# A conv-attention and mixture-of-experts network on one core: the order of the last norm, of the late expert blocks, of the last additions and of the first matmuls

## The chip, the cores and the metric

The kernel runs on one core of a Trainium2 chip. The metric is the device time of one execution in microseconds (us). A core has a matmul engine (TensorE, PE in the profile; its weight loads are PEld), three engines for elementwise work (VectorE is DVE, ScalarE is ACT, GpSimd is POOL) and SyncE (SP), which only issues DMA transfers here. Each engine works through its own queue in order, and waits on semaphores for the others.

## The reference

The input `x` is 8 images of 256 channels and 32 x 32 = 1024 positions (tokens). All is float32.

```python
# layer 0, for each image, 8 heads of 64
qkv = xt @ w_qkv + b_qkv
attn = softmax(q @ k^T * 64**-0.5, axis=query)
t = (attn @ v) @ w_out + b_out + xt
# layer 1
n = layernorm(t)                       # over the 256 channels
t = t + softmax((n @ W^T) @ n^T) @ n   # 1024 x 1024 scores
n = layernorm(t)
gates = top 2 of softmax(n @ router_w^T), normed to sum 1
y = n + sum over 8 experts of gate_e * (gelu(n @ w1[e] + b1[e]) @ w2[e] + b2[e])
out = t + y                            # turned back to channels
```

## The kernel before

The images go one after the other. `layer0` computes the first layer of an image in 32 steps, each of one pair of heads and one block of 128 keys: scores into PSUM (`psc`), two maxima on DVE (`first_max`, `second_max`), the exponential on ACT (`soften`), the values divided by the sums on DVE (`divide`, which writes `vs`), and the product with the values into `po` (`gather_values`). Between PE's parts of a product stand empty instructions on another queue (`relay`): on POOL's for image 0, on SP's for the others. Then `pr` multiplies by `w_out` and adds to the residual `t1`, which `residual` has made of the input (turned on DVE) and the bias (added on POOL).

`attend` is the second attention. It norms `t1` into `n1` (class `Norm`: statistics block by block, square root on ACT, reciprocal, writes), turns `n1` to channels (`to_channels`: PE transposes and two DVE copies), and mixes eight blocks of queries; at named places it calls `fill`, where other work is put in. `normed` does the second norm and its turn.

The experts are handled in two ways. For images 0 to 6 each token's normed row is scattered to its two experts' lists in DRAM (`dispatch`, one scatter in a step of the next image's layer 0). After layer 0 of image 7, `experts` runs 63 blocks of 256 rows: `fetch` loads a block (SP), `stage` copies its weights (ACT), `turned` transposes it (`xb`, DVE), `hidden` multiplies by `w1` (`ph`) and applies gelu, `collect` multiplies by `w2` (`pe`), adds the bias, scales by the gate and scatters the rows to `y` (POOL). Two buffers hold `xb`, four hold weights. The last four blocks are handed to `fill` and finished within image 7's attention. Image 7's own experts are computed in `dense`: for each of 8 experts and 2 halves of the tokens, `pdh`, gelu, `pdy`, and four gated adds to `t2` on DVE.

Beside `dense`, `Results` ends the other seven images: 14 halves, for each of which a sum and two results are loaded (512 KB each), added on DVE (`add`), transposed on DVE into one of two buffers `oT` and stored (`store`). `tick`, called after each dense step, stores the half added before and adds the next:

```python
def tick(self, k, behind):
    if self.stored < self.added:
        self.store()
    if self.added < len(self.todo):
        self.add(behind)
```

The order on each engine is set by a scheduler with a cost model of its own; `tc.issue_after(x)` places what is issued within it behind the instruction `x` in the order, and `add_manual_dep` makes it wait.

At the start the first input halves and weights are loaded, three idle matmuls run, and `Begin.all` computes the values of six token blocks (`pv`, two contraction halves `cc` each), with small PE transposes of biases and routers (`ps_bqk`, `ps_W`, `ps_r`, `ps_rs`, `ps_b1`) between.

## Time and profile before

| | us |
|---|---|
| median of 3 runs | 2308.49 (2308.31 to 2310.03) |
| the profiled execution's own time | 2309.37 |
| its span in the profile | 2307.6 |
| PE busy | 2248.4 |
| DVE busy | 1567.6 |
| ACT busy | 1238.8 |
| POOL busy | 313.6 |

The span is that of the instructions; the execution's own time takes in what lies around it. In lines of the timeline the columns are start, duration, engine, line, operation, out<-in, count, and in brackets the idle time before it with what ended it. In lines of waits they are the waiting engine and line, what it waited for, total us, times, longest. Counts of matmuls are of records: a float32 matmul leaves two.

### The profile page before, as it was taken

What the parts mean: (1) busy time and instruction counts of PE and PEld (TensorE: products, weight loads), DVE (VectorE), ACT (ScalarE), POOL (GpSimd) and SP (SyncE); (2) the same over time, 40 slices, a digit from 0 to 9 for tenths busy, and PEclk for the clock granted to TensorE, in tenths of its full rate; (3) what the DMA queues carried; (4) which work ended last, traced back from release to release, by engine and by line L of the source; (5) the groups of instructions that cost most, each with busy time, mean ns of one, the idle gap of its engine ahead of it and who ended that gap; (6) DMA issues with size and microseconds to landing.
All of it is one profiled execution on the core that took longest, in us unless ns stands there. A gap on an engine that the chain in (4) does not pass through costs nothing.

```text
span 2307.6 us, 38039 instructions
## 1 busy us (share of the span) xinstructions
PE 2248.4 (97%) x13061; PEld 1213.5 (53%) x13061; DVE 1567.6 (68%) x3922; ACT 1238.8 (54%) x2221; POOL 313.6 (14%) x313
## 2 busy tenths in 40 slices
PE   9999999999999999999999999999999989999996
PEld 3345633563456335643554355534553468885664
DVE  4776688557865786578757775677668955556575
ACT  3664566356635663656474656466446645556311
POOL 1000012000200030003000200021001225551100
PEclk9999999999999999999999999999999999999998
DMA  8996201020103010201021101100050146651475
GB/s 277 356 348 189 50 17 40 7 57 11 47 1 63 6 52 1 45 19 52 6 37 27 45 13 21 43 20 20 14 123 17 40 86 147 147 143 42 167 216 156
DMA packets 277177, 182.82 MB, mean 79 GB/s; under 512 B 194564, under 2 KB 232247, under 8 KB 275960
## 3 DMA queue, kind: packets, MB, share of 16 engines
q1 hardware_dynamic: 264264, 150.08, 24.3%
q0 software_dynamic: 11632, 29.78, 3.6%
q8 instruction: 104, 1.70, 0.3%
q14 instruction: 89, 0.73, 0.1%
q10 hardware_dynamic: 1088, 0.52, 0.1%
HBM read 63.47 MB, written 106.61 MB: 74 GB/s over the span
## 4 chain that ended last, share of the span: by engine, by line
PE 83%; DVE 5%; ACT 5%; SPq 4%; issue 2%; DMA 1%; POOL 0%; DVEq 0%; ACTq 0%; POOLq 0%
PE po L587 19%; PE psc L510 19%; PE pqk L380 7%; PE py L897 7%; PE pr L689 5%; PE pv L417 4%; PE ph L1332 3%; PE ps L791 3%; PE pe L1359 3%; PE pdy L1547 2%; PE px L728 2%; PE pdh L1524 2%; SPq L880 2%; PE pqk L358 2%; PE ps1z L791 2%
## 5 line engine op out<-in xcount | busy, mean ns | idle before, releaser
L551 ACT ACTIVATE ex<-psc,nmax 128x1024 f32<-128x1024 f32 x512 | 570.0, 1114 | 301.4 <-DVE scrap L534 218.5
L510 PE MATMUL psc<-qk,qk 64*64 64x512 f32 x4096 | 576.0, 592 | 4.3 <-ACT ex L551 4.1
L587 PE MATMUL po<-ex,vs 64*64 64x512 f32 x4096 | 570.6, 591 | 3.5 <-DVE vs L567 2.4
L534 DVE TENSOR_SCALAR_CACHE_REDUCE scrap<-psc,nmax 128x512 f32<-128x512 f32 x512 | 384.4, 751 | 158.7 <-PE psc L510 130.5
L525 DVE TENSOR_REDUCE nmax<-psc 128x1 f32<-128x512 f32 x512 | 350.6, 685 | 9.3 <-PE psc L510 9.3
L510 PEld LDWEIGHTS psc<-qk,qk 64*64 64x64 f32 x4096 | 179.7, 132 | 281.8 <-ACT ex L551 133.1
L587 PEld LDWEIGHTS po<-ex,vs 64*64 64x64 f32 x4096 | 175.0, 132 | 277.5 <-DVE vs L567 82.9
L1149 POOL DMA_INDIRECT rows<-n,d_at x112 | 109.1, 974 | 515.8 <-DVE nmax L525 479.8
L380 PE MATMUL pqk<-xT,wqkv 128*128 128x512 f32 x384 | 171.2, 599 | 0.0
L1380 POOL DMA_INDIRECT y<-yb,to x126 | 123.6, 981 | 191.7 <-DVE yb L1374 165.4
L345 ACT ACTIVATE qk<-pqk,b_qks 128x512 f32<-128x512 f32 x124 | 85.5, 690 | 88.9 <-PE pqk L380 79.8
L417 PE MATMUL pv<-wqkv,xT 128*128 128x512 f32 x256 | 121.7, 600 | 2.2 <-ACT wqkv L121 1.3
L380 PEld LDWEIGHTS pqk<-xT,wqkv 128*128 128x128 f32 x384 | 71.0, 190 | 99.9 <-issue 77.3
L1332 PE MATMUL ph<-xb,w_ring 128*128 128x256 f32 x488 | 117.2, 384 | 4.5 <-DVE xb L1321 4.5
L880 ACT COPY spare<-home 32x256 f32<-32x256 f32 x272 | 109.4, 402 | 17.4 <-DVE home L868 11.9
L689 PE MATMUL pr<-wo,res 128*128 128x256 f32 x512 | 113.6, 383 | 2.0 <-ACT res L606 2.0
L897 PE MATMUL py<-n,spare 128*128 128x256 f32 x512 | 114.9, 379 | 0.0
L1141 POOL IOTA n<- 128x8 f32 x14 | 2.0, 142 | 829.6 <-PE py L897 829.6
L1359 PE MATMUL pe<-w_ring,hb 128*128 128x256 f32 x472 | 111.6, 379 | 0.0
L689 PEld LDWEIGHTS pr<-wo,res 128*128 128x128 f32 x512 | 98.4, 192 | 19.6 <-ACT res L606 6.0
L897 PEld LDWEIGHTS py<-n,spare 128*128 128x128 f32 x512 | 96.5, 190 | 20.1 <-issue 4.3
L1332 PEld LDWEIGHTS ph<-xb,w_ring 128*128 128x128 f32 x488 | 93.6, 192 | 18.5 <-DVE xb L1321 5.7
(262 smaller groups left out, 2795.2 us busy)
## 6 DMA issues: line engine op xcount, KB each, us to landing
rows<-zero SPq DMA_DIRECT2D x7, 8256.0 KB
xr<-rows SPq DMA_DIRECT2D x252, 64.0 KB
xs<-in_x_dram SPq DMA_DIRECT2D x64, 128.0 KB
ys<-y SPq DMA_DIRECT2D x16, 512.0 KB
spare<-home SPq DMA_DIRECT2D x240, 32.0 KB
out_dram<-oT SPq DMA_DIRECT2D x60, 128.0 KB
xT<-in_x_dram SPq DMA_DIRECT2D x7, 1024.0 KB
sums<-t SPq DMA_DIRECT2D x7, 1024.0 KB
```

Source lines behind the costliest of these rows:

```text
L380: mm = nc.tensor.matmul(pq[:, ts(n, 512)], wqkv[:, cc, t, ts(g, P)], xT[:, cc, ts(n, 512)], start=(cc == 0), stop=(cc == NCC - 1),)
L417: nc.tensor.matmul(pv, self.xT[:, cc, ts(i, P)], wqkv[:, cc, 2, :], start=(cc == 0), stop=(cc == NCC - 1),)
L510: mm = nc.tensor.matmul(pss[at, h][ts(c, DK), ts(n, 512)], k[r, j * P + c * DK : j * P + (c + 1) * DK], q[r, ts(n, 512)], start=True, stop ...
L525: firsts[at, h] = nc.vector.tensor_reduce(nmax, pss[at, h][:, ts(0, 512)], AX.X, ALU.max, negate=True)
L534: seconds[h] = nc.vector.tensor_scalar(scrap, pss[at, h][:, ts(1, 512)], -1.0, nmaxes[at, h], ALU.mult, ALU.min, accum_out=nmax,)
L551: nc.scalar.activation(ex, pss.pop((at, h)), AF.Exp, bias=nmaxes.pop((at, h)), scale=1.0, accum_out=sums[at][:, h : h + 1],)
L587: mm = nc.tensor.matmul(po[n][ts(h, DK), :], vss[at][keys, h, :], exps[at, h][keys, ts(n, 512)], start=(j == 0 and turn == 0), stop=(j == ...
L689: nc.tensor.matmul(pr[:, :C], res[g][:, ts(i, P)], wo[:, g, :], start=(g == 0), stop=(g == NPAIR - 1))
L880: move(to[ts(k, SQ), a], since[ts(a, SQ), k])
L897: evicted["mixed"] = nc.tensor.matmul(py[:, :D], aT[m], n1[:, m, :], start=(m == 0), stop=(m == NT - 1))
L1332: last = nc.tensor.matmul(ph[:, ts(fc, BR)], wb[:, dc * FF + fc * P : dc * FF + (fc + 1) * P], xb[:, dc, :], start=(dc == 0), stop=(dc == ...
L1359: mm = nc.tensor.matmul(py[:, ts(r, D)], hT[:, fc, ts(r, P)], wb[:, ts(fc, D)], start=(fc == 0), stop=(fc == NFC - 1),)
```

## The change

1. Start: the `cc = 0` matmuls of all six `pv` blocks are issued first, and the transposes of `b_rows` and `W_rows` are placed behind them.
2. `residual`: POOL's bias add is cut into two halves, each behind the `divide` of one of the two following steps, for every image.
3. Last attention: its norm is no longer done before `attend` but in 23 steps, one behind each of the first expert blocks (four empty, eight of statistics, square root, one empty, reciprocal, eight writes). Weight copies are placed behind the last gelu, and before there is one, behind the last copy of `res`.
4. Late blocks: block `end - 2` is finished before the last turn of the attention instead of at the second norm. Of block `end - 1` the bias add stays there, and the scaling and scatters come behind the norm's two copies to channels; POOL's adds of the normed tokens come behind the scaling.
5. Dense stage: a tick adds a half and transposes and stores it at once, behind the step's gated adds, and the next step's gated adds are placed behind that transpose. The last half of image 7 is transposed and stored in two parts.

```diff
+    bigs = [big(f"pv_0_{i}") for i in range(0, 6, 2)]
+    first_pvs = [bigs[i // 2][:, ts(i % 2, 512)] for i in range(6)]
+    for i, pv in enumerate(first_pvs):
+        opened = nc.tensor.matmul(
+            pv, next_x[:, 0, ts(i, P)], wqkv[:, 0, 2, :], start=True, stop=False
+        )
...
-        nc.tensor.transpose(ps[:, ts(t, NPAIR)], b_rows[:, t, :], ident[:NPAIR, :NPAIR])
+        with tc.issue_after(opened.ins):
+            nc.tensor.transpose(ps[:, ts(t, NPAIR)], b_rows[:, t, :], ident[:NPAIR, :NPAIR])
...
-        nc.gpsimd.tensor_add(t1, t1, b_o.unsqueeze(1).to_broadcast([P, NT, C]))
-        return t1
+        def bias(n, behind):
+            some = t1[:, ts(n, NB), :]
+            added = nc.gpsimd.tensor_add(some, some, b_o.unsqueeze(1).to_broadcast([P, NB, C]))
+            tc.add_manual_dep(added.ins, behind.ins.name, BEHIND)
+
+        return t1, [lambda behind, n=n: bias(n, behind) for n in range(NH2)]
...
                 with tc.issue_after(seconds[0].ins):
                     ahead = divide(at - 1) if at > 0 else seconds[0]
+                    if parts and at > 0:
+                        parts.pop(0)(ahead)
...
-        tick("turned", to_channels(tokens, nT, f"n2_{b}"))
+        copied = to_channels(tokens, nT, f"n2_{b}")
+        tick("turned", copied)
...
+            with tc.issue_after(copied.ins):
+                fill("turned")
...
-                    tc.add_manual_dep(added.ins, written.ins.name, BEHIND)
+                    tc.add_manual_dep(added.ins, evicted["scaled"].ins.name, BEHIND)
...
         def stage(b):
+            with tc.issue_after((gelus[-1] if gelus else evicted["copied"]).ins):
+                copy_weights(b)
...
                 collect(b - 4, hiddens.pop(b - 4), last, squares)
+                if steps:
+                    with tc.issue_after(evicted["scaled"].ins), tc.issue_after(gelus[-1].ins):
+                        steps.pop(0)()
...
-        def tick(self, k, behind):
-            if self.stored < self.added:
-                self.store()
+        def tick(self, behind):
             if self.added < len(self.todo):
-                self.add(behind)
+                self.store(self.add(behind))
...
+        def part(at):
+            turned = nc.vector.transpose(
+                oT[:, :, ts(at, P // parts)].rearrange("p g (i t) -> p i g t", i=some),
+                total[:, ts(at, some), :].rearrange("p i (g c) -> p i g c", c=SQ),
+            )
+            for a in range(NQ):
+                queue = nc.scalar if b == B - 1 and a % 2 else nc.sync
+                queue.dma_start(
+                    dst[n, a][:, :, ts(at, P // parts)], oT[ts(a, SQ), :, ts(at, P // parts)]
+                )
+            return turned
...
+                with tc.issue_after(others.last.ins) if others.last else nullcontext():
+                    for j in range(2):
...
+                if (e, n) == (E - 1, NH2 - 1):
+                    if i == 0:
+                        ending = store(b, t2[:, ts(n, NB), :], n, 2)
+                    with tc.issue_after(added.ins):
+                        others.last = ending(i // 2)
+            others.tick(added)
+            if (e, n) == (E - 1, 0):
+                with tc.issue_after(added.ins):
+                    others.last = store(b, t2[:, ts(n, NB), :], n)
...
+        n1 = one.tile([P, NT, D], F32, tag="n", name=f"n1_{b}")
+        n1_norm = Norm(t1, n1, 1e-5, f"a{b}")
+        steps = [lambda: None for _ in range(4)]
+        steps += [lambda i=i: n1_norm.stats(i, i + 1) for i in range(NT)]
+        steps.append(lambda: n1_norm.root(0, NT))
+        steps.append(lambda: None)
+        steps.append(lambda: n1_norm.invert(0, NT))
+        steps += [lambda i=i: n1_norm.write(i, i + 1) for i in range(NT)]
+        product, result = experts(groups[0], evicted["divided"], table, steps)
...
+            elif place == "last weights 2":
+                result(end - 2)
             elif place == "norm 2":
                 with tc.issue_after(evicted["mixed"].ins):
-                    result(end - 2)
-                    result(end - 1)
+                    sends = result(end - 1, False)
+            elif place == "turned":
+                for send in sends:
+                    evicted["sent"] = send()
```

More of the change, by code (lines that the diff above doesn't have):

```diff
@@ L220 @@
         for dc in range(NCC):
-            nc.tensor.transpose(
-                ps[:, dc * D + ec * P : dc * D + (ec + 1) * P], W_rows[:, ec, ts(dc, P)], ident
-            )
+            with tc.issue_after(opened.ins):
+                nc.tensor.transpose(
+                    ps[:, dc * D + ec * P : dc * D + (ec + 1) * P], W_rows[:, ec, ts(dc, P)], ident
+                )
     WT = const.tile([P, NCC, D], F32, name="WT")
@@ L268, in __init__, with stats @@
             self.rstd = small.tile([P, NT], F32, tag="rstd", name=f"rstd_{name}")
-        def blocks(self, first, end):
-            t, mv, rstd = self.t, self.mv, self.rstd
+        def stats(self, first, end):
+            t, mv = self.t, self.mv
             for i in range(first, end):
@@ L277, in blocks, with root, write @@
                 nc.vector.bn_aggr(mv[:, i, :], st)
-            some = rstd[:, first:end]
+        def root(self, first, end):
+            mv, some = self.mv, self.rstd[:, first:end]
             nc.vector.tensor_scalar_add(some, mv[:, first:end, 1], self.eps)
             nc.scalar.activation(some, some, AF.Sqrt)
-            nc.vector.reciprocal(some, some)
+        def write(self, first, end):
+            t, mv, rstd = self.t, self.mv, self.rstd
             for i in range(first, end):
@@ L295, in blocks, with invert @@
             return written
+        def invert(self, first, end):
+            some = self.rstd[:, first:end]
+            nc.vector.reciprocal(some, some)
+        def blocks(self, first, end):
+            self.stats(first, end)
+            self.root(first, end)
+            self.invert(first, end)
+            return self.write(first, end)
     def layer_norm(t, dst, eps, name):
@@ L402, in __init__, with open, product @@
             self.todo = list(range(NT))
+        def open(self):
+            if self.v is None:
+                self.v = one.tile([P, NT, INNER], F32, tag="v", name=f"v_{self.b}")
+        def product(self, pv, i, cc):
+            return nc.tensor.matmul(
+                pv,
+                self.xT[:, cc, ts(i, P)],
+                wqkv[:, cc, 2, :],
+                start=(cc == 0),
+                stop=(cc == NCC - 1),
+            )
         def values(self, n, single=False):
             b = self.b
-            if self.v is None:
-                self.v = one.tile([P, NT, INNER], F32, tag="v", name=f"v_{b}")
+            self.open()
             now, self.todo = self.todo[:n], self.todo[n:]
@@ L416, in values @@
                 for cc in range(NCC):
-                    nc.tensor.matmul(
-                        pv,
-                        self.xT[:, cc, ts(i, P)],
-                        wqkv[:, cc, 2, :],
-                        start=(cc == 0),
-                        stop=(cc == NCC - 1),
-                    )
+                    self.product(pv, i, cc)
             for i, pv in zip(now, pvs):
@@ L437, in at, with all @@
                     self.project(True)
-            if place not in ("between 2", "last products"):
+            if place not in ("between 2", "last weights 2", "last products", "turned"):
                 self.values(1)
-        def all(self):
-            for _ in range(3):
-                self.values(2)
+        def all(self, pvs):
+            self.open()
+            now, self.todo = self.todo[: len(pvs)], self.todo[len(pvs) :]
+            for i in now:
+                self.product(pvs[i], i, 1)
+            for i in now:
+                nc.vector.tensor_add(self.v[:, i, :], pvs[i], b_v)
             for _ in range(2):
@@ L501, in layer0 @@
         po, copied, counted = None, None, None
+        parts = []
         def score(at, h, n):
@@ L611, in gather_values @@
                 ]
+                evicted["copied"] = copied[-1]
             return mm
@@ L671, in layer0 @@
                     with tc.issue_after(ahead.ins):
-                        t1 = residual(b, xs)
+                        t1, parts = residual(b, xs)
                 if g == 0:
@@ L693, in layer0, with attend @@
         return t1
-    def attend(b, t1, fill, tick=nothing):
+    def attend(b, t1, fill, tick=nothing, n1=None):
         spare = [
@@ L703, in attend @@
         SQ_AT = {1: (3, None), 2: (0, 7), 3: (1, 6), 4: (0, 1), 5: (4, 7), 6: (5, 6)}
-        n1 = one.tile([P, NT, D], F32, tag="n", name=f"n1_{b}")
-        layer_norm(t1, n1, 1e-5, f"a{b}")
+        if n1 is None:
+            n1 = one.tile([P, NT, D], F32, tag="n", name=f"n1_{b}")
+            layer_norm(t1, n1, 1e-5, f"a{b}")
         fill("norm 1")
@@ L951, in attend @@
         mix(*sixth)
+        fill("last weights 2")
         now = turn_now(7, eighth[1])
@@ L1248, in plan, with experts @@
         yield placed
-    def experts(group, behind, table):
+    def experts(group, behind, table, steps):
         n = group.n
@@ L1285, in experts, with copy_weights @@
         spare = two.tile([P, LATE // 2, WE], F32, tag="xT", name="w_late")
-        firsts, seconds = {}, {}
+        firsts, seconds, gelus = {}, {}, []
         W1 = NCC * FF
         def stage(b):
+            with tc.issue_after((gelus[-1] if gelus else evicted["copied"]).ins):
+                copy_weights(b)
+        def copy_weights(b):
             late = b - (group.nb - LATE // 2)
@@ L1342, in hidden @@
             for fc in range(NFC):
-                nc.scalar.activation(
-                    hT[:, fc, :],
-                    ph[:, ts(fc, BR)],
-                    AF.Gelu,
-                    bias=b1T[:, bass.ds(at + fc, 1)],
-                    scale=1.0,
+                gelus.append(
+                    nc.scalar.activation(
+                        hT[:, fc, :],
+                        ph[:, ts(fc, BR)],
+                        AF.Gelu,
+                        bias=b1T[:, bass.ds(at + fc, 1)],
+                        scale=1.0,
+                    )
                 )
@@ L1366, in collect, with add @@
             yb = two.tile([P, R, D], F32, tag="yb", name=f"yb_{n}_{b}")
-            with tc.issue_after(squares.ins) if squares else nullcontext():
-                nc.vector.tensor_add(
+            def add():
+                return nc.vector.tensor_add(
                     yb,
@@ L1372, in collect, with send @@
                 )
+            if squares is not None:
+                with tc.issue_after(squares.ins):
+                    add()
+                    send(b, yb)
+            return mm, add, yb
+        def send(b, yb):
+            if True:
                 where = wheres.pop(b)
-                nc.vector.tensor_mul(yb, yb, where[:, :, 0:1].to_broadcast([P, R, D]))
+                scaled = nc.vector.tensor_mul(yb, yb, where[:, :, 0:1].to_broadcast([P, R, D]))
+                evicted["scaled"] = scaled
                 to = small.tile([P, R], I32, tag="to", name=f"to_{n}_{b}", bufs=4)
@@ L1379, in collect @@
             for r in range(R):
-                nc.gpsimd.indirect_dma_start(
+                sent = nc.gpsimd.indirect_dma_start(
                     out=group.ways[R * b + r][:, :],
@@ L1387, in collect @@
                 )
-            return mm
+            return sent
         rows, hiddens, wheres = {}, {}, {}
@@ L1403, in experts @@
                 collect(b - 4, hiddens.pop(b - 4), last, squares)
+                if steps:
+                    with tc.issue_after(evicted["scaled"].ins), tc.issue_after(gelus[-1].ins):
+                        steps.pop(0)()
+        assert not steps
         for b in range(group.nb - LATE, group.nb - LATE // 2):
@@ L1409, in product, with result @@
             return mm
-        def result(b):
-            return collect(b, hiddens.pop(b), None, None)
+        def result(b, whole=True):
+            mm, add, yb = collect(b, hiddens.pop(b), None, None)
+            if whole:
+                add()
+                return send(b, yb)
+            return add, lambda: send(b, yb)
         return product, result
@@ L1434, in __init__ @@
             self.sent, self.added, self.stored = 0, 0, 0
+            self.last = None
             for _ in self.slots:
@@ L1455, in add, with store @@
                 for k in range(2):
-                    nc.vector.tensor_add(total, total, self.slots[at][:, k])
-        def store(self):
+                    added = nc.vector.tensor_add(total, total, self.slots[at][:, k])
+            return added
+        def store(self, behind):
             at = self.stored % len(self.slots)
@@ L1461, in store @@
             self.stored += 1
-            store(self.group.items[n], self.totals[at], h)
+            with tc.issue_after(behind.ins):
+                self.last = store(self.group.items[n], self.totals[at], h)
             self.load()
-        def tick(self, k, behind):
-            if self.stored < self.added:
-                self.store()
+        def tick(self, behind):
             if self.added < len(self.todo):
-                self.add(behind)
-    def store(b, total, n):
+                self.store(self.add(behind))
+    def store(b, total, n, parts=1):
         oT = two.tile([P, D // SQ, P], F32, tag="qk1", name=f"oT_{b}_{n}")
-        nc.vector.transpose(
-            oT.rearrange("p g (i t) -> p i g t", i=NB),
-            total.rearrange("p i (g c) -> p i g c", c=SQ),
-        )
         dst = out[b].rearrange("(g c) (n a k) -> n a c g k", c=SQ, n=NH2, a=NQ)
-        for a in range(NQ):
-            queue = nc.scalar if b == B - 1 and a % 2 else nc.sync
-            queue.dma_start(dst[n, a], oT[ts(a, SQ)])
+        some = NB // parts
+        def part(at):
+            turned = nc.vector.transpose(
+                oT[:, :, ts(at, P // parts)].rearrange("p g (i t) -> p i g t", i=some),
+                total[:, ts(at, some), :].rearrange("p i (g c) -> p i g c", c=SQ),
+            )
+            for a in range(NQ):
+                queue = nc.scalar if b == B - 1 and a % 2 else nc.sync
+                queue.dma_start(
+                    dst[n, a][:, :, ts(at, P // parts)], oT[ts(a, SQ), :, ts(at, P // parts)]
+                )
+            return turned
+        if parts > 1:
+            return part
+        return part(0)
     def dense(b, t2, norm, fill, begin, table):
@@ L1553, in collect @@
                         )
-                for j in range(2):
-                    block = n * (NT // NH2) + i + j
-                    added = nc.vector.scalar_tensor_tensor(
-                        t2[:, block, :],
-                        py[:, ts(j, D)],
-                        all_gates[:, block, e : e + 1],
-                        t2[:, block, :],
-                        ALU.mult,
-                        ALU.add,
-                    )
-            others.tick(e * NH2 + n, added)
-            if e == E - 1:
-                store(b, t2[:, ts(n, NB), :], n)
+                with tc.issue_after(others.last.ins) if others.last else nullcontext():
+                    for j in range(2):
+                        block = n * (NT // NH2) + i + j
+                        added = nc.vector.scalar_tensor_tensor(
+                            t2[:, block, :],
+                            py[:, ts(j, D)],
+                            all_gates[:, block, e : e + 1],
+                            t2[:, block, :],
+                            ALU.mult,
+                            ALU.add,
+                        )
+                if (e, n) == (E - 1, NH2 - 1):
[7 more added lines that the diff above has]
+                    others.last = store(b, t2[:, ts(n, NB), :], n)
         pending = None
@@ L1579 @@
     begun = Begin(0, next_x)
-    begun.all()
+    begun.all(first_pvs)
     xs = load_squares(0)
@@ L1599 @@
             continue
-        product, result = experts(groups[0], evicted["divided"], table)
-        norm = None
+        n1 = one.tile([P, NT, D], F32, tag="n", name=f"n1_{b}")
+        n1_norm = Norm(t1, n1, 1e-5, f"a{b}")
[6 more added lines that the diff above has]
+        product, result = experts(groups[0], evicted["divided"], table, steps)
+        norm, sends, sent = None, [], None
         end = groups[0].nb
         def fill(place):
-            nonlocal norm
+            nonlocal norm, sends
             if place == "between":
@@ L1624, in fill @@
                 return norm.blocks(0, NT - 1)
-        t2 = attend(b, t1, fill)
+        t2 = attend(b, t1, fill, nothing, n1)
         dense(b, t2, norm, fill, lambda: Results(groups[0]), table)
```

## The prediction

> **What bounds the kernel now.** I read the page's busy shares first, then what TensorE (PE) waited for, then the chain of waits from 2286 us on, and last the granted clock by stage, because that chain is PE for 83% of the span.

> ```profile
> PE 2248.4 (97%) x13061; PEld 1213.5 (53%) x13061; DVE 1567.6 (68%) x3922; ACT 1238.8 (54%) x2221; POOL 313.6 (14%) x313
> PE ph L1332 <- DVE xb L1321: 4.0, 2, 3.6
> PE pr L689 <- ACT res L606: 2.0, 1, 2.0
> ```

> PE is the bound, so an edit pays only where PE stands still, or before its first and after its last matmul. The two waits are those of 1850 to 1885 us, where the last image passes from attention to the expert blocks. The next fence is what the engines did there.

> ```profile
> 1849.75 3.88 ACT L1294 COPY w_ring<-table 128x1024 f32 x4 [0.56 <-DVE vs L567]
> 1854.17 15.77 PE L689 MATMUL pr<-wo,res 128*128 128x256 f32 x64 [1.98 <-ACT res L606]
> 1874.19 1.28 ACT L280 ACT_TABLE_LOAD   x1
> 1876.13 2.67 DVE L287 TENSOR_SCALAR n<-t,mv_a,rstd_a 128x256 f32<-128x256 f32 x8 [0.20 <-DVE rstd_a L281]
> 1879.48 3.58 PE L1332 MATMUL ph<-xb,w_ring 128*128 128x256 f32 x8 [3.63 <-DVE xb L1321]
> ```

> Four weight copies stand ahead of the copy of `res`, and pr starts late. Then the norm's square root, with table loads on both sides, and its eight writes stand on DVE ahead of the transpose `xb`, and PE idles 3.63 us. The end of the kernel, from the chain of waits:

> ```profile
> 2286.91 0.48 DVE t L1556
> 2293.45 2.49 DMA out_dram<-oT
> 2298.67 2.52 DMA out_dram<-oT
> 2301.36 1.25 DVE oT L1474
> ```

> PE is done at 2286.5 of 2307.6. The last 21 us are six transposes and two adds that the order on DVE left behind, each transpose waiting for the store that frees one of two buffers `oT`. The clock, by stretches (columns: PE, weight loads, DVE, ACT, POOL busy; granted clock; DMA share; GB/s):

> ```profile
> 1852.31:1855.72 3.41, 1.55 (x7) 1.34 (x8) 0.00 (x0) 2.29 (x4) 0.00 (x0) 0.96 0.11 22
> 1855.70:1858.60 2.90, 2.90 (x8) 2.37 (x7) 1.03 (x3) 0.00 (x0) 0.00 (x0) 0.50 0.59 106
> 1879.60:1882.70 3.10, 3.10 (x8) 2.47 (x9) 1.75 (x4) 0.00 (x0) 1.39 (x2) 0.50 0.40 85
> 2162.84:2166.25 3.41, 2.55 (x12) 0.83 (x12) 3.19 (x2) 0.00 (x0) 3.41 (x3) 1.00 0.00 0
> 2169.70:2172.60 2.90, 2.90 (x6) 1.33 (x5) 0.67 (x3) 1.55 (x3) 1.73 (x2) 0.50 0.03 1
> ```

> After three idle stretches PE runs at half clock for some 3.4 us, which costs about 1.7 us beside the gap itself. A fourth such stretch, at 2190, follows the matmuls of the biases and stays.

> **The change part by part.** The sum is made against the profiled execution: 2309.37 us, of which the span is 2307.6. It is 0.9 above the median of the runs, 2308.49, so I take 0.9 off at the end.

> *Start.* PE stops from 10.4 to 11.18 us for `b_rows`, a DMA. Now three more `pv` matmuls of 0.86 us stand before that wait, and the transposes come behind. PE's work is the same, so the stop goes: **-0.8**. Late next would be the DVE copy of the second half of `wqkv`, begun at 10.86 and wanted only near 14.

> *Bias on POOL.* The row for both sides:

> ```profile
> 1796.52 4.53 POOL L472 TENSOR_TENSOR t<-t,b_o 128x2048 f32<-128x2048 f32 x1 [4.62 <-DVE t L468]
> 1798.68 2.52 DVE L567 TENSOR_TENSOR vs<-v,rs 128x128 f32<-128x128 f32 x1
> 1801.26 1.09 PE L587 MATMUL po<-ex,vs 64*64 64x512 f32 x8 [1.74 <-DVE vs L567]
> ```

> In the last image DVE's product of two SBUF inputs took 2.52 instead of 0.29 us, until POOL's add ended, and PE lost 1.74. In two halves, 2.26 each, begun behind one `vs` and ended before the next (3.44 later), it blocks none: -1.7. In the other seven images it ran beside the projection and cost nothing; the halves now stand in steps where DVE's other operations read PSUM, and those kept 0.7 us beside POOL at 1797. In image 0 alone PE also waits for empty instructions in POOL's queue, and these now stand behind a half: from `vs` at 116.99 to 119.3, against a matmul at 119.05. That is 0.3 to 0.4 twice, or nothing if the queue passes them on while the add runs. No row tells; I take +0.4, with 0 and 0.8 kept. In images 1 to 6 each half also delays a row scatter in POOL's queue, for which nobody waits before the next image. Net **-1.3**.

> *Norm among the expert blocks, copies behind.* `res` is copied as soon as po ends at 1852.19: 0.1 for the signal and 0.53 for the first copy, so pr starts near 1852.85 instead of 1854.17 (-1.3). pr then keeps full clock: 64 records at 0.216 are 13.8 instead of the 15.6 to the first ph (-1.8). From there to the end of the third ph took 13.29 (1869.77 to 1883.06); four groups of 1.73 are 6.9 (-6.4). In all **-9.5**. Who is late next: `xb` of the third block needs the first ph and 0.7 us of DVE, ready 2.7 before its use; the first gelu has its table loaded early, since ACT is free; the weight copy of block 2 (1.04) stands behind that gelu and is ready 2 before use. SP's fetches (five issues, 2.2 us a block against 3.45) are not moved.
> The moved work: in a block DVE now does transpose 0.70, add 0.69, multiply 0.69, index 0.16 and one step, at most 0.43 + 0.18. At 2066 us `xb` was ready 1.2 before its matmul, so 0.55 is left; it would cost (x - 0.55) a block if a step took longer. The square root puts two table loads of 1.28 between two gelus: a gelu's result is used 3.45 after its matmul and needs 0.84 + 1.28 + the rest of a copy. Covered, once.

> *Clock.* [...] But in the row of 1852.31 PE was busy 1.55 of 3.41 us and half clock followed, while 2.55 of 3.41, at 2162.84, was let pass. I go by the rows: what is left at pr's start is two gaps of 0.7, at least 2.4 busy in any 3.4.

> *Late blocks.* Before, on DVE:

> ```profile
> 2162.31 1.23 DVE L321 COPY n2T<-pt_n 128x1024 f32<-128x1024 f32 x1 [0.47 <-PE pt_n L320]
> 2163.45 2.58 DVE L1374 TENSOR_TENSOR yb<-yb,where 128x512 f32<-128x512 f32 x1
> 2166.79 0.69 DVE L1368 TENSOR_TENSOR yb<-pe,b_all 128x512 f32<-128x512 f32 x1 [0.76 <-POOL t L1066]
> 2167.40 1.21 DVE L321 COPY n2T<-pt_n 128x1024 f32<-128x1024 f32 x1
> ```

> The second copy comes directly behind the first. Against it, one block's `pe` (1.73) moves from the wait for the norm to before turn 7, where PE is full, so all behind it is 1.73 later. Second copy: the last norm write ends at 2161.24 + 1.73 = 2162.97, transposes 0.4, two copies 1.2 each: 2165.8. The logits matmuls end at 2166.6 with one pdh done, before 2169.3 with two: 2.7 - 0.86 = 1.8 gained. Two waits, 0.9 and 1.2, remain here; whether they halve the clock hangs on where the window falls, so half of 1.7. **-2.6** (0.5 to 3.5). POOL's adds (2.06, 2.06 and two short) now come behind the scatters and lie over the gates' chain, whose products of two SBUF inputs they hold up as `vs` was: the gates come near 2178 against 2177.2 wanted, and PE has two PSUM buffers, some 5 us, as cover.

> *Dense stage.* A step of PE is 3.43 + 3.45 = 6.88. DVE in fixed order: four gated adds, then two adds 2.47, transpose 1.25. At 2193.52 to 2199.72 the same work took 6.2, so 0.7 is left, and PE feels a late DVE only after 5. A step moves 1.5 MB in and 0.5 out; 356 GB/s at 2207 us and about 240 for stores (193 at a share of 0.80) make 4.4 + 2.2 = 6.6 us, with loads five halves ahead. The end: last matmul 2286.5, two gated adds 0.9, half a transpose 0.70 (the row of `xb`, same size), and 5.0 from there to the end of the span as now: 2293.1, **-14.5**. The last half is now stored in runs of 256 bytes. [...] The nearest row is the 64 KB load `xr`, also in runs of 256 bytes, 1.68 us to land at 2060.58. By the row the half would save 0.8 of 2.5[...].

> Sum: 0.8 + 1.3 + 9.5 + 2.6 + 14.5 = 28.7. 2309.4 - 28.7 - 0.9 = **2279.8**.

> **The rivals.**
> *The gap comes back among the blocks (0.12).* The 9.5 us in which SP and ACT ran ahead are gone; if fetch or `xb` is then late, only pr's 3.1 and part of the rest remain. Against it: 1.2 us of slack at `xb`. -9.5 becomes -4: 2285.
> *The tail shrinks by half (0.10).* DVE in fixed order waits for loads or for `oT` and arrives late at the last step by 7 us: 2287; with both rivals 2292.
> *Slower (0.04).* DMA sets the pace of the dense stage. It averaged 215 GB/s there; if that is its ceiling and not its demand, a step needs 2.1 MB / 215 = 9.75 us, 14 steps lose 40, less 5 of cover: 2315. It decides for slower from a step of 9.3 us on ((28.7 + 5) / 14 above 6.88). Against it: 356 to 397 GB/s in several slices.
> *It does not do what it says (0.02).* The orders of both programs show each move, so only effects could cancel.

> **How the numbers follow.** Likeliest 0.72, its own range 2276 to 2284, from the bounds above. To leave out no more than 2 in 10 the range reaches into the two milder rivals: 2275 to 2289. 0.2%, 4.6 us, is what a measurement tells from none. Faster 0.93, same 0.03, slower 0.04.

> **What would show it.** Right: pr's wait for `res` and the 3.63 us at ph gone, no half clock between 1850 and 1890; one DVE `n` write per block; the two n2T copies touching; `oT` beside every dense step; under 8 us from the last matmul to the end. Wrong: waits of ph for `xb`, of DVE `total` or `oT` for DMA inside the dense stage, or of po for POOL's queue in image 0 beyond 1 us.

## The result, and the profile after

| | median, us | runs | ratio to before, 95% interval |
|---|---|---|---|
| before | 2308.71 | 2308.31 to 2310.03 (4) | |
| changed | 2287.72 | 2285.63 to 2289.62 (4) | 0.9908 [0.9891, 0.9925] |

The change makes the kernel 21.0 us faster. The forecast was 28.9 (2308.7 - 2279.8): inside the stated range, but beyond the likeliest case's own 2276 to 2284. The profiled execution of the changed kernel took 2285.63 us, the fastest of its four, with a span of 2283.8, 23.8 below the span of before.

First the page's busy row of the changed kernel, then what its PE waited for (us in total, times, longest).

```profile
PE 2243.0 (98%) x13061; PEld 1211.9 (53%) x13061; DVE 1568.4 (69%) x3923; ACT 1233.7 (54%) x2221; POOL 316.5 (14%) x321
```

```profile
PE pdy L1630 <- DVE t L1640: 4.0, 2, 2.0
PE pdh L1607 <- ACT dh L1616: 2.8, 2, 1.4
...
PE ph L1383 <- DVE xb L1372: 0.9, 1, 0.9
...
PE pr L731 <- ACT res L645: 0.7, 1, 0.7
```

Of the two waits that carried the prediction, the 3.6 us of `ph` are gone (the 0.9 above is another wait, at 2058.64 us), and the 2.0 of `pr` are down to 0.7. The first two lines are new, and both stand in the dense stage, where PE had no wait before. Where the last image passes to the expert blocks, the timeline of PE reads as predicted:

```profile
1848.57 14.08 PE L731 MATMUL pr<-wo,res 128*128 128x256 f32 x64 [0.68 <-ACT res L645]
1862.49 3.62 PE L1383 MATMUL ph<-xb,w_ring 128*128 128x256 f32 x16
1865.94 1.89 PE L1412 MATMUL pe<-w_ring,hb 128*128 128x256 f32 x8
1867.67 1.89 PE L1383 MATMUL ph<-xb,w_ring 128*128 128x256 f32 x8
```

`pr` runs at full clock (1.00 granted from 1847.20 to 1861.30), and three `ph` and one `pe` follow without a stop. The end of the dense stage reads otherwise:

```profile
2231.31 6.17 PE L1607 MATMUL pdh<-n2T,table 128*128 128x512 f32 x14
2237.32 3.62 PE L1630 MATMUL pdy<-table,dh 128*128 128x256 f32 x16
2242.35 3.70 PE L1607 MATMUL pdh<-n2T,table 128*128 128x512 f32 x8 [1.42 <-ACT dh L1616]
2245.89 3.62 PE L1630 MATMUL pdy<-table,dh 128*128 128x256 f32 x16
2250.92 3.70 PE L1607 MATMUL pdh<-n2T,table 128*128 128x512 f32 x8 [1.42 <-ACT dh L1616]
2254.46 7.07 PE L1630 MATMUL pdy<-table,dh 128*128 128x256 f32 x32
2263.56 8.90 PE L1630 MATMUL pdy<-table,dh 128*128 128x256 f32 x32 [2.04 <-DVE t L1640]
2274.43 3.69 PE L1630 MATMUL pdy<-table,dh 128*128 128x256 f32 x16 [1.96 <-DVE t L1640]
```

One half step is 8 `pdh` and 16 `pdy`. Here 14 `pdh` stand in one group and five half steps of `pdy` stand at the end with no `pdh` between them; before, `pdh` and `pdy` alternated to the end and two were left:

```profile
2275.97 3.60 PE L1524 MATMUL pdh<-n2T,table 128*128 128x512 f32 x8
2279.40 7.07 PE L1547 MATMUL pdy<-table,dh 128*128 128x256 f32 x32
```

With `pdy` alone PE takes 3.45 us a half step, and DVE's timeline shows 5.2 for its share, back to back:

```profile
2261.41 1.25 DVE L1551 STREAM_TRANSPOSE oT<-total 128x1024 f32<-128x1024 f32 x1
2262.58 1.62 DVE L1640 SCALAR_TENSOR_TENSOR t<-pdy,all_gates,t 128x256 f32<-128x256 f32 x4
2264.12 2.47 DVE L1529 TENSOR_TENSOR total<-total,ys 128x1024 f32<-128x1024 f32 x2
2266.62 1.25 DVE L1551 STREAM_TRANSPOSE oT<-total 128x1024 f32<-128x1024 f32 x1
```

The sum of the two spans, from starts of the same matmuls in both (minus is gained):

| part | predicted | in the two profiles |
|---|---|---|
| start, at the first `pqk` (20.72 to 19.81) | -0.8 | -0.9 |
| bias, images 0 to 6 | +0.4 | -1.5 |
| bias, image 7 | -1.7 | -1.9 |
| norm and copies, to the first `px` of the last attention | -9.5 | -8.8 |
| late blocks, to the first `pdy` | -2.6 | -3.2 |
| first `pdy` to the last matmul (109.2 to 118.0, less 0.9 for two `pdh` moved into it) | 0 | +7.9 |
| last matmul to the end (21.1 to 5.7) | -14.5 | -15.4 |
| sum | -28.7 | -23.8 |

The dense row is 7.9 us off. The bias in images 0 to 6 is 1.9 off, on the good side, and the others are within 0.9.

### The profile page after: what moved, and what is told of

The parts are those of the page before. It is cut to its first block, busy times and chain, and to the rows that moved or that the text cites. A ratio compares the mean times of both kernels' runs of the same rounds, so it can differ in the third digit from the quotient of the medians.

```text
span 2283.8 us, 38057 instructions
## 1 busy us (share of the span) xinstructions
PE 2243.0 (98%) x13061; PEld 1211.9 (53%) x13061; DVE 1568.4 (69%) x3923; ACT 1233.7 (54%) x2221; POOL 316.5 (14%) x321
## 4 chain that ended last, share of the span: by engine, by line
PE 77%; issue 8%; ACT 4%; DVE 4%; POOL 3%; SPq 2%; DMA 2%; POOLq 0%; DVEq 0%; ACTq 0%
PE po L626 19%; PE psc L549 19%; PE pqk L402 7%; PE py L940 7%; PE pr L731 4%; PE pv L432 4%; PE ps L834 3%; POOL y L1444 3%; PE pdh L1607 2%; PE px L771 2%; SPq L923 2%; PE pqk L380 2%; PE pdy L1630 2%; PE ps1z L834 2%; ACT aT L923 1%
## 5 line engine op out<-in xcount | busy, mean ns | idle before, releaser
L1196 POOL DMA_INDIRECT rows<-n,d_at x112 | 109.2, 975 | 462.7 <-DVE nmax L564 424.5
L432 PE MATMUL pv<-wqkv,xT 128*128 128x512 f32 x244 | 116.4, 600 | 1.0 <-DVE v L454 1.0
L1395 ACT ACTIVATE hb<-ph,b1T 128x256 f32<-128x256 f32 x126 | 52.8, 471 | 108.1 <-PE ph L1383 103.6
```

Source lines behind the costliest of these rows:

```text
L432: return nc.tensor.matmul(pv, self.xT[:, cc, ts(i, P)], wqkv[:, cc, 2, :], start=(cc == 0), stop=(cc == NCC - 1),)
```

## The experiments

Each kernel was timed beside the kernel before on the same chip. There were three chips, on which the kernel before had medians of 2308.30, 2308.01 and 2308.01, which agree within 0.3 us, so medians of different chips can be compared. But executions of one kernel differ by up to 8.3 us here, so effects under 3 us are read in the profiles, by stage, and not from the medians.

| run | edit | median, us | runs | ratio to before |
|---|---|---|---|---|
| pin | changed kernel, PE's order alternating | 2279.47 | 2276.7 to 2282.3 | 0.9879 [0.9864, 0.9894] |
| nodense | changed kernel, dense part undone | 2297.06 | 2291.9 to 2297.3 | 0.9942 [0.9928, 0.9955] |
| pin_freedve | pin, DVE's order free | 2293.28 | 2291.2 to 2295.7 | 0.9938 [0.9924, 0.9951] |
| pin_whole | pin, last store in one piece | 2282.39 | 2279.2 to 2283.4 | 0.9889 [0.9874, 0.9904] |
| pin_pb | pin, bias matmuls spread | 2278.95 | 2276.1 to 2280.1 | 0.9877 [0.9861, 0.9894] |
| pin_nonorm | pin, norm in one piece | 2281.45 | 2280.0 to 2287.1 | 0.9884 [0.9868, 0.9901] |
| pin_nocopies | pin, weight copies ahead again | 2281.66 | 2277.5 to 2285.9 | 0.9891 [0.9873, 0.9909] |
| pin_nolate | pin, late blocks as before | 2279.83 | 2279.6 to 2283.0 | 0.9884 [0.9867, 0.9900] |
| pin_early | pin, POOL's adds behind the norm | 2276.77 | 2275.2 to 2278.5 | 0.9867 [0.9851, 0.9884] |
| pin_pb_early | pin, bias matmuls spread and POOL's adds behind the norm | 2276.91 | 2276.2 to 2277.7 | 0.9869 [0.9852, 0.9885] |
| pin_nobias | pin, one long add on POOL | 2284.76 | 2283.6 to 2285.6 | 0.9903 [0.9887, 0.9920] |
| pin_nostart | pin, start as before | 2280.23 | 2277.3 to 2283.9 | 0.9878 [0.9861, 0.9894] |

### PE's order in the dense stage

The instruction order of the changed program (hidden layer `h`, output `y`, expert and half):

```
before:   y3,0  h4,0  y3,1  h4,1  y4,0  h5,0  y4,1  h5,1 ...             h7,1  y7,0  y7,1
changed:  y3,0  h4,0  h4,1  y3,1  h5,0  h5,1  h6,0(1 of 4)  y4,0  ...    h7,1  y5,1  y6,0  y6,1  y7,0  y7,1
```

The diff has no line about this: the scheduler places PE's instructions. The first run pins the alternation and moves nothing else: in the two traces the instructions of DVE, ACT, POOL and SP stand in the same order.

```diff
-        def hidden(e, n):
+        def hidden(e, n, behind):
...
+                    with tc.issue_after(behind.ins) if behind else nullcontext():
                         nc.tensor.matmul(ph[:, ts(fc, 512)], ...)
...
-            now = (e, n, hidden(e, n))
+            now = (e, n, hidden(e, n, behind if at > 3 else None))
...
-                collect(*pending)
+                behind = collect(*pending)    # its last matmul
```

> The changed kernel, with one addition: in the last dense stage the matmuls of the hidden layer (pdh) of step k+2 are queued on PE behind the output matmuls (pdy) of step k, so that the two alternate as they did before the change; DVE, ACT, POOL and SP keep the order of the changed kernel. Theory A (PE's order): in the changed kernel six groups of pdh stand earlier on PE than before, so that the last steps consist of pdy alone, 3.45 us a step, against 5.4 us of DVE a step; PE lost 1.42 + 1.42 + 2.04 + 1.96 in waits and 1.83 in a half-clock window, 8.7 together. With the alternation they go: 2285.6 - 8.7 = 2277 us, waits of pdy for t and of pdh for dh gone, last matmul near 2269. Theory B (DVE's fixed order): DVE waits for loads or for oT whatever PE's order is; then the time stays at 2285 to 2289 with the same waits.

Measured: 2279.47, 8.2 below the changed kernel's median; the profiled execution took 2276.79. In the dense stage PE has no wait, the last matmul ends at 2268.85 (theory A: near 2269), and the end of its timeline is

```profile
2261.78 7.07 PE L1631 MATMUL pdy<-table,dh 128*128 128x256 f32 x32
```

DVE then waits for PE, not PE for DVE, in the same fixed order:

```profile
2254.96 1.25 DVE L1551 STREAM_TRANSPOSE oT<-total 128x1024 f32<-128x1024 f32 x1
2256.82 0.88 DVE L1641 SCALAR_TENSOR_TENSOR t<-pdy,all_gates,t 128x256 f32<-128x256 f32 x2 [0.61 <-PE pdy L1631]
```

Theory B, that DVE in fixed order is late for its own reasons, falls. (The expectation speaks of six groups of `pdh`; the order above shows that at the end `pdh` is three half steps further ahead of `pdy` than before.)

The next run takes the dense part out of the changed kernel, without a pin: the hunks of `Results`, `store` and `collect` undone.

> The changed kernel with the last part undone: the adds and turns of the other images stand in the dense stage as they did before (an add per step, a turn in the next one, no order given on DVE, the last store in one piece). Theory A: PE's stream alternates again, so the 8.7 us lost in the stage go, and the 21 us tail returns in place of 5.7: 2285.6 - 8.7 + 15.4 = 2292 us. Theory C (the loss in the dense stage belongs to the other parts, such as POOL's late adds to t): the 8.7 stay and the time is 2301 us.

Measured: 2297.06, between A's 2292 and C's 2301, so the time alone doesn't choose. The profile does:

```profile
2162.45 3.87 PE L1619 MATMUL pdy<-table,dh 128*128 128x256 f32 x16 [1.72 <-ACT dh L1605]
...
2267.34 7.07 PE L1619 MATMUL pdy<-table,dh 128*128 128x256 f32 x32
```

Between these two lines PE alternates without a wait, neither for `t` nor for `dh`, and 21.0 us lie behind the last matmul at 2274.4. That is A. The last matmul is later than in the pinned run (2268.85) by 5.6 us for other reasons, two of which are taken up below: the wait of 1.72 for the first `dh`, and half clock ahead of it (granted clock 0.50 from 2150.63 to 2154.05). That the scheduler alternates in this program and not in the changed one shows that the dense part's edit brought the new PE order; why the scheduler chose it stays open.

The third run keeps PE pinned and drops DVE's fixed order.

```diff
-                with tc.issue_after(others.last.ins) if others.last else nullcontext():
+                with nullcontext():
...
-            with tc.issue_after(behind.ins):
+            with nullcontext():
                 self.last = store(self.group.items[n], self.totals[at], h)
```

> As the run with the alternating PE order, but without the fixed order on DVE: the scheduler places adds and turns, and leaves five turns behind the last matmul's adds. Theory A and the prediction (the tail is DVE's order, 14.5 us): about 2277 + 15 = 2292 us, with the chain of turn, store, turn at the end. Rival (the tail came from PE's order, and the fixed order on DVE brings nothing of its own): 2277 us.

Measured: 2293.28. PE ends as early as in the pinned run (7.07 us from 2261.68), and the chain of waits behind it is the old one:

```profile
2275.73 2.50 DMA out_dram<-oT
...
2278.31 1.26 DVE oT L1551
...
2280.95 2.54 DMA out_dram<-oT
...
2283.66 0.71 DVE oT L1551
```

So the fixed DVE order is what removes the tail (behind the last matmul 20.8 us without it and 6.2 with it, 13.8 between the two medians), and the new PE order is what it costs. The last store in one piece:

```diff
-                if (e, n) == (E - 1, NH2 - 1):
-                    if i == 0:
-                        ending = store(b, t2[:, ts(n, NB), :], n, 2)
...
-            if (e, n) == (E - 1, 0):
+            if e == E - 1:
```

> As the run with the alternating PE order, but the last half of the last image is turned and stored in one piece (runs of 512 bytes) instead of two (runs of 256 bytes). The turn is 1.25 instead of 0.71 us at the end: +0.5. By the row of the 64 KB load the store also takes 2.5 instead of 1.7: +1.3 in all. [...]

Measured by stage: from the last matmul to the end 7.0 us (2270.4 to 2277.4) against 6.15 pinned (2268.85 to 2275.0), +0.9. The turn's 0.54 is in it, so the store in two parts with runs of 256 bytes saves about 0.3. The other profiles bear this out: from the end of the last turn to the end of the span it is 4.55 to 4.95 us in the four that store the last half in one piece, and 4.04 to 4.48 in the ten that store it in two, 0.4 less in the mean. The row of `xr` said 0.8, and the prediction's sum counted none; what was measured lies between, so the half in 256-byte runs did not take as long as the whole. The medians differ by 2.9 us, which the tail does not explain.

### The other parts, undone one by one

The norm in one piece again (`steps = []`, and `attend` makes its own norm):

> As the run with the alternating PE order, but the last attention's norm stands again in one piece between the last product and the late blocks, as before the change; the weight copies stay behind the copy of res and the gelus. By the prediction's working the PE time from the end of pr to the end of the third ph goes from 6.9 to 13.3 us: +6.4, with a wait of ph for xb of about 3.6 us and a half-clock window. Rival (the norm only waited for ACT's weight copies, so the copies alone bring it): +0 to +1.

```profile
1862.49 1.89 PE L1383 MATMUL ph<-xb,w_ring 128*128 128x256 f32 x8
1867.16 2.55 PE L1383 MATMUL ph<-xb,w_ring 128*128 128x256 f32 x8 [2.77 <-DVE xb L1372]
1869.51 3.03 PE L1412 MATMUL pe<-w_ring,hb 128*128 128x256 f32 x8
1872.37 1.89 PE L1383 MATMUL ph<-xb,w_ring 128*128 128x256 f32 x8
```

From the first `ph` to the end of the third: 11.77 us against 7.07, +4.7, of which 2.8 is the wait and 1.8 the half clock behind it (2.55 and 3.03 for 1.89). The rival's +0 to +1 falls by the wait alone. The medians differ by 2.0 only: the profiled execution is the slowest of its four, and how much half clock the others had is not known. The prediction's +6.4 was for norm and copies together; the copies undone alone:

```diff
-            with tc.issue_after((gelus[-1] if gelus else evicted["copied"]).ins):
-                copy_weights(b)
+            copy_weights(b)
```

> As the run with the alternating PE order, but the weight copies are no longer queued behind the copy of res and the gelus: four copies stand again ahead of res on ACT. Theory of the prediction (by the rows of before): pr starts 1.3 us later after a wait of 2.0 and runs its first 3.4 us at half clock (1.8 more): +3.1. [...] If the ring of weights then runs ahead again and relieves the first blocks, less.

```profile
1849.50 14.08 PE L731 MATMUL pr<-wo,res 128*128 128x256 f32 x64 [1.99 <-ACT res L645]
1863.42 3.62 PE L1382 MATMUL ph<-xb,w_ring 128*128 128x256 f32 x16
1867.50 1.99 PE L1411 MATMUL pe<-w_ring,hb 128*128 128x256 f32 x8 [0.47 <-ACT hb L1394]
```

The wait of 1.99 is back (+1.3), and `hb` adds 0.5, but `pr` keeps full clock in this execution (1.00 from 1851.29 to 1854.70). From the end of `po` (1847.51) to the end of the third `ph` (1871.22) it is 23.7 us, against 21.7 in the changed kernel (1847.89 to 1869.56): +2.0. Norm 4.7 and copies 2.0 make 6.7 of the 9.2 us that lie between before (30.9) and changed. Of the other 2.5, 1.7 are the half clock in `pr` that this execution did not have (15.6 us from `pr` to the first `ph` before, 13.9 here), and most of the rest is that `ph` waited longer for `xb` before (3.63 against 2.77 without the norm's part).

The late blocks as before the change:

> As the run with the alternating PE order, but the last two blocks' results both stand again at the second norm, with their scaling on DVE between the two copies of n2T. By the prediction's working +2.6 (0.5 to 3.5): the wait of the second logits group for n2T, 2.5 us, comes back, less one block's pe of 1.7 us that covers part of it, and the clock may halve behind it. Rival (the wait is covered by pdh matmuls that can run first): 0.

```profile
2154.01 0.64 PE L1009 MATMUL pl<-n2T,rTs 128*32 128x256 f32 x8 [2.53 <-DVE n2T L343]
```

The wait of 2.53 is back, and the first `pdy` begins at 2162.61 against 2158.80 in the pinned run; less the two `pdh` done earlier (0.9) that is +2.9. Half clock in `pdh` is put at 1.5 of it, an estimate from a window of 3.41 us at 2152.13 in which PE was busy for 1.53. Yet the median is only 0.4 above the pinned run's. What it wins back is told in the next part.

One long add on POOL:

> As the run with the alternating PE order, but POOL adds b_o in one instruction of 4.5 us again. By the prediction: +1.3 to 1.7, all of it in the last image, where vs takes about 2.5 us instead of 0.3 and po waits 1.7 for it. Rival (the small stops of 0.1 to 0.4 us that the changed kernel no longer had in images 2 to 6, 1.5 us together, came from the long add): +3, with PE about 1.5 us later at the begin of the last image.

```profile
1798.08 2.53 DVE L600 TENSOR_TENSOR vs<-v,rs 128x128 f32<-128x128 f32 x1
...
1800.67 1.98 PE L620 MATMUL po<-ex,vs 64*64 64x512 f32 x8 [1.76 <-DVE vs L600]
```

`vs` and PE's wait are there as predicted, with a half-clock window behind them this time (granted clock 0.50 from 1800.24 to 1803.66; before, 1.00 from 1800.81 to 1804.22). The rival is right as well: before the last image PE is 1.8 us later than pinned (1607.86 against 1606.04 at the last `pr` before it), in small stops in images 1 to 6. At the last `pr` it is 5.2 later (1853.54 against 1848.37), and the medians differ by 5.3. The stops are not at the add: one of them, before, is DVE idle for 0.47 us at 810.67 where it is 0.19 elsewhere, 18 us ahead of that image's add. Nor is it the order on the other engines: that of DVE, ACT and SP is the same in both traces, and PE's differs in twelve records of layer 0. What links the stops to the add stays open.

The start:

> As the run with the alternating PE order, but the first value matmuls are issued as before the change, behind the wait for b_rows. By the prediction: +0.8, with PE's stop of 0.8 us near 10.4 and the first pqk at 20.7 instead of 19.8. Rival (the stop moves to another load, such as wqkv): 0.

```profile
PE ps_bqk L211 <- DMA b_rows<-in_L_conv_b_qkv_dram: 0.6, 1, 0.6
```

The first image's `pr` begins at 169.18 against 168.49: +0.7, where 0.8 was predicted; the medians cannot tell it.

### The spread: clock windows and POOL's adds

Three profiles (nodense, pin_nonorm, pin_nostart) share one thing that the others lack: the first `pdy` waits 1.7 to 1.8 us for `dh`. The timeline of DVE in the last of them, and then of DVE and POOL in the pinned run:

```profile
2157.77 3.92 DVE L1023 TENSOR_TENSOR g_p<-g_l,g_m 128x64 f32<-128x64 f32 x1
```

```profile
2154.36 0.23 DVE L1042 TENSOR_TENSOR g_p<-g_l,g_m 128x64 f32<-128x64 f32 x1
...
2155.40 4.47 DVE L1048 TENSOR_TENSOR g_p<-g_p,g_z 128x64 f32<-128x64 f32 x1
...
2155.23 4.13 POOL L1113 TENSOR_TENSOR t<-t,n 128x896 f32<-128x896 f32 x2
```

Where POOL's adds come late, behind the scaling, one DVE product of two SBUF inputs takes 3.9 to 4.5 us and ends only after the first two of them: 4.45 in the changed kernel, 4.47 in the pinned run, 4.44 in pin_nobias, 3.92 in pin_nostart, for the 0.23 of such a product elsewhere. In the pinned profile the gates' subtraction (0.23) is 0.9 us ahead of them and a later product pays, which nobody but the gated adds waits for. Where PE's logits come later, the subtraction itself is caught (3.92), and behind it ACT's exp, the table load, the gelus `dh` and `pdy`. And in all three PE was busy for only 1.34 to 1.39 us of one window of 3.41 on the two waits before the logits (1.34 in nodense from 2147.22, 1.39 in pin_nonorm from 2151.70, 1.34 in pin_nostart from 2149.03). In nodense and pin_nostart half clock is read in the next 3.41 us, and the logits come later there. The rows (columns: length, PE busy, granted clock, DMA share, GB/s; first the run with the old start, then pinned):

```profile
2149.03:2152.44 3.41, 1.34 (x16) 1.00 0.00 0
2152.44:2155.85 3.41, 3.41 (x18) 0.50 0.00 0
```

```profile
2148.31:2151.72 3.41, 1.89 (x12) 1.00 0.00 0
2151.72:2155.14 3.42, 3.42 (x17) 1.00 0.01 0
```

The same two waits, but the windows cut them differently: behind the one with 1.34 us busy the granted clock was 0.50, behind the one with 1.89 it was 1.00. Two edits test this. The first moves only POOL's adds:

```diff
-                    tc.add_manual_dep(added.ins, evicted["scaled"].ins.name, BEHIND)
+                    tc.add_manual_dep(added.ins, written.ins.name, BEHIND)
```

> As the run with the alternating PE order, but POOL's adds of the norm to t stand behind the last norm write, as before the change, and not behind the scaling of the last block; nothing else moves. They should run from about 2148.7 to 2153.7, beside the two copies of n2T, whose input is PSUM. Theory (POOL's add blocks DVE's products of two SBUF inputs, and in the runs near 2282 us it does so to the gates' subtraction, ahead of ACT's exp and gelus, so that pdy waits 1.8 us for dh): the product g_p of 4.47 us takes 0.23, the first gated add begins 3 to 4 us earlier, no wait of pdy for dh, and the runs near 2282 become fewer: median near 2277. Against it: yb's product then waits for POOL until 2153.7 instead of ending at 2152.7, and the gates begin up to 1 us later. Rival (the gates are covered by two PSUM buffers and the spread is the clock alone): same median and spread, 2277 to 2282.

```profile
2148.65 4.10 POOL L1113 TENSOR_TENSOR t<-t,n 128x896 f32<-128x896 f32 x2 [8.00 <-DVE n_last L299]
...
2154.28 0.23 DVE L1042 TENSOR_TENSOR g_p<-g_l,g_m 128x64 f32<-128x64 f32 x1
...
2155.32 0.23 DVE L1048 TENSOR_TENSOR g_p<-g_p,g_z 128x64 f32<-128x64 f32 x1
...
2160.71 0.88 DVE L1641 SCALAR_TENSOR_TENSOR t<-pdy,all_gates,t 128x256 f32<-128x256 f32 x2 [1.60 <-PE pdy L1631]
```

No product is held up (only the small `to<-where`, with one SBUF input, takes 0.98 instead of 0.16), the first gated add comes at 2160.71 instead of 2163.55, and no run is above 2278.5: the median is 2276.77. The two faster executions of the pinned run took the same time, 2276.7 and 2276.8; what this run lacks is executions like the pinned run's other two, of 2282. The intervals of this and the pinned run overlap (0.9867 and 0.9879); the profile and the spread speak for it, the medians alone don't prove it. It fits pin_nolate, whose adds stood early too: between its median and this one, not the pinned one, lie 3.1 us.

The second spreads the bias matmuls `pb`, after which before and the pinned run show half clock (0.50 from 2189.93 and from 2172.20, for 3.41 us): one group between each two groups of `pdh` or `pdy`.

> As the run with the alternating PE order, but the four groups of bias matmuls (pb, 8 rows of weights, 0.86 to 0.97 us each), which stood in one block of 3.9 us, are spread: one between each two groups of pdh or pdy. PE's work is the same. Theory ([...]a window that falls on the block is followed by 3.4 us at half clock): the window behind pb, 1.8 us, goes from the profile, and no granted clock of 0.50 between 2165 and 2180; the median falls by 1 to 2 us. Rival (the window at 2172 was brought by the waits of 2148 to 2151 or by chance): the same number of half-clock windows and the same time.

```profile
2170.06 1.12 PE L1598 MATMUL pb<-b_rows,gT 8*128 8x256 f32 x4
2171.11 3.70 PE L1613 MATMUL pdh<-n2T,table 128*128 128x512 f32 x8
```

The half-clock window went as expected: from 2169 to 2185 the granted clock is 1.00, where the pinned run had

```profile
2168.79:2172.20 3.41, 3.41 (x17) 1.00 1.02 396
2172.20:2175.60 3.40, 3.40 (x9) 0.50 1.08 317
```

But only 0.7 us of the 1.8 stays: PE reaches the same `pdh` (behind the fourth `pdy`) at 2188.75 instead of 2189.48. The first of the four groups takes 1.05 us up to the next matmul, where a group of the pinned block takes 0.96 (3.83 for four); the rest of the 1.1 us in between was not shown. The median fell by 0.5, which is no difference. Both together:

> Both additions to the run with the alternating PE order: spread bias matmuls, and POOL's adds behind the last norm write. If both theories hold, the half-clock window after pb and the wait for dh are both gone: 2275 to 2277 us with little spread. If neither is worth anything in time: 2279 with the same spread.

2276.91, the narrowest spread of all (1.6 us), and the same as the adds alone. Either version beats both kernels: about 31 us below before and 11 below the changed kernel.

## Why the prediction was right or wrong

**Right.** The start (-0.8; 0.9, and 0.7 when undone). `pr` without the four copies (-1.3; 1.3). The half clock at `pr` and in the third `ph` (-1.8 and a part of -6.4; 1.7 and 6.2). The second copy of `n2T` behind the first (-2.6; 3.2). The tail (-14.5; 15.4: behind the last turn 4.0 us are left where 5.0 were taken).

**The step that failed** is the sentence "A step of PE is 3.43 + 3.45 = 6.88" of the dense stage. It took PE's alternation of `pdh` and `pdy` from the profile of before and put a new DVE order beside it. With five half steps of `pdy` left at the end, a step of PE is 3.45, DVE's 5.2 is the longer, and "PE feels a late DVE only after 5" has no ground. The waits (6.8) and a half-clock window (1.8) are 8.7 us, less 1.8 for the window behind `pb` that this execution lacked (granted clock 1.00 from 2168 to 2188); 1.0 of the 7.9 is left in smaller pieces. The pinned run, in which the sentence holds, has a median of 2279.47. The sentence in the rivals, "the orders of both programs show each move", was false in the same place: the move of `pdh` was in the order of the changed program and had been overlooked. The rival "the tail shrinks by half" had nearly this time (2287), but not this mechanism: no load and no `oT` was late, and the tail went whole. So it is luck that the median lies in the stated range: the range reached to 2289 for the sake of two rivals, and neither of them is what happened.

**Mis-sized.** The long add was put at nothing in images 1 to 6; it costs 1.5 to 1.8 us there, by a way that stays open. The empty instructions of image 0 (+0.4) cost nothing: PE is 0.91 ahead of before on both sides of them. The norm part lost 0.5 to a new wait of `xb`, 0.88, near its end. That "the gates come near 2178 against 2177.2 wanted" put them 0.8 us late; in the changed kernel they end 4.6 us behind the start of the first `pdy`. The two PSUM buffers covered this too, but the sentence looked at one reader only. The other, exp and the gelus behind it on ACT, has no cover when POOL's add comes first (in pin_nostart the first `pdy` waited 1.8 us for `dh`). The pinned kernel's executions of 2282 beside those of 2277 look like it (granted clock 0.997 against 0.998 and 0.999); no profile of them exists, so that is argued, not shown. The 6.2 us read for DVE's work of a step held 0.85 of waiting for PE; back to back it is 5.2. And of the six transposes in the tail of before, four waited for a store, not each.

**The half clock.** The rows were the right guide: half clock followed windows of 3.41 us in which PE was far from idle, busy for 1.43 us (before), 1.38 (changed) and 1.23 (pin_nonorm). By the rows the part of norm and copies was -9.5; at the end of the third `ph` the two profiles give -9.2. But the rows gave too much certainty: at the same wait of 2.0 before `pr` half clock followed before (1.43 busy in the window, whose begin the prediction's row of 1852.31 did not meet), and not in the run with the copies ahead (1.79 busy).

## What to carry to other kernels

Where a scheduler places the instructions, an order fixed on one engine can change the order on another: compare the instruction order of each engine over the whole stage, above all of the one that bounds it, before taking its step time from the old profile. If the order was what made the overlap work, write it down. And when an add on POOL is moved, list every DVE product that it can hold up (here one of 0.23 us took up to 4.47) and all that come behind it, not only the nearest.
